# Reordering the turns of a four-layer cross-attention kernel: quotients first, row normalisation on ScalarE

## The chip, the cores and the metric

The kernel runs on one core of a Trainium2 chip. The metric is the device time of one execution in microseconds, the median of several. The core's engines are TensorE (PE; its weight loads are listed apart as PEld), VectorE (DVE), ScalarE (ACT) and GpSimd (POOL). SyncE (SP) issues most of the transfers.

## What is computed

The input x has shape (4, 256, 256): four sequences of 256 tokens with 256 features. Four layers follow each other, and each adds an attention and then a feed-forward part to x:

```python
x = x + xattn(layernorm(x), ctx)      # 16 heads; keys and values are 512 rows of 128 from ctx
x = x + ffn(layernorm(x))             # a different ffn in each layer
```

The attentions of layers 1 to 3 have the form that matters here (layer 0's is smaller and is not touched):

```python
q = (x @ Wq).reshape(B, T, 16, 128); k, v = ctx @ Wk, ctx @ Wv     # 8 key/value groups
out = (softmax(q k^T / sqrt(128)) @ v) @ Wo
```

The feed-forward parts after them are a mixture of eight experts of which each token takes two (layer 1), a choice between two experts (layer 2), and a router that lets 64 tokens of each sequence through an expert (layer 3).

## The kernel before

**Folded weights.** `folding` multiplies Wq with Wk into `m_sb` and Wv with Wo into `n_sb` for each head, in PSUM, and copies the products to SBUF. The copies of the second product are L1006 (64 partitions, two heads) and L1008 (64 partitions, one head, twice).

**The order.** Inside `manual_schedule` each engine executes its instructions in the order of the program text; only the DMA queues are apart. An attention goes through 32 turns, called units: sequence b = 0 to 3, and within it head pair hp = 0 to 7. A turn contains, in this order, pieces of work that belong to different units:

- at hp 1 the statistics of the next sequence's rows (`Norm`), at hp 3 their normalisation (`tokens`, L926);
- the next unit's query products (PE to banks paq and pbq, then L1861 to L1865);
- `row_sums` (L1925, L1926) of the unit that is held back, if there is one;
- `summed` of the previous unit on VectorE (L1978 add, L1980 transposition, L1984 reduction): the denominators of the softmax;
- `exponentials` of this unit: scores on PE into bank "s", exponentials on ScalarE (L1900) into pT;
- at i = 0 (hp 0 and 4) the output products of a finished group of four units;
- `after(b, hp)`: a piece of the following feed-forward part;
- at i = 1 (hp 1 and 5) `quotients` of the last finished group: PE sums into pz (L1993), VectorE inverts (L1999, L2000), multiplies into rr (L2003), reduces (L2004, L2005) and sets signs (L2009);
- for an even hp with b > 0 (a coded unit, but for the second last of a layer): half sums and differences on POOL (L1914, L1920), and the unit is held back for the next turn. For every other unit: `plain` products on PE (L1938 to L1940) into po, copied by ScalarE (L1941);
- at i = 1 and 2 `divided`: VectorE spreads the inverses (L2015, tile wide), POOL multiplies (L2016);
- if a unit is held: `seven_values`, which finishes it with seven products instead of eight: pva on PE (L1950 to L1955), two ScalarE operations (L1956, L1957), pvb on PE (L1963), four VectorE operations (L1967 to L1971). There are 33 such turns, 11 in each layer: hp odd, b > 0, except hp = 7 of b = 3. After it come this unit's own half sums on POOL.

**PSUM banks.** Tiles get banks by tag, in turn: "s" has four, "mm" two, "t" one and "o" one. Scores and output products use "s", queries "mm". The one bank "t" is shared by pz, pva, transposed rows, the routers' small products, and layer 3's gathered rows. The one bank "o" is shared by po and pvb:

```python
pa = bank("t", [P, 2, S], f"pva{L}_{b}_{hp}")
pb = bank("o", [P, 2, S], f"pvb{L}_{b}_{hp}")
```

**The pieces in `after`.** `beside1` (layer 1): for b = 0 it issues waiting weight loads; for b > 0 it does the feed-forward's `Norm` at hp 4, `tokens` at hp 5, transposition at hp 6 and `chosen` at hp 7 (logits pl on PE in bank "t", then some twenty small VectorE operations, L2238 to L2263, and one ScalarE exponential L2244). `beside2` (layer 2) has the same at hp 4 and 5, sends the normalised rows to memory (xd2, on SP's queue), and lets `taken_by` read them; at the last two turns it ranks the tokens and gathers rows with indirect transfers on POOL (L2782). `beside3` (layer 3) does the router: `Norm` at hp 4; `tokens`, `weight` (L3075) and `weights` at hp 5; `spread` and `places` at hp 6 and 7; for b > 1 `gathered` at hp 1 (PE products pxg L3142 in bank "t", copied to xgT by L3149) and `rest` at hp 2 (L3132). With b = 0 it issues loads and takes a step of `bounds` at hp 3, 5 and 7.

The functions of the change with their lines:

Of the kernel before, what the change touches and what calls it, by code (L numbers as in the profile page):

```python
# [12 lines left out]
AF = mybir.ActivationFunctionType  # L13
ALU = mybir.AluOpType
# [3 lines left out]
P = 128  # L18
B, S, D = 4, 256, 256
NC = S // P  # L20
ND = D // P
# [17 lines left out]
KSEL = 64  # L39
# [797 lines left out]
def bounded_path(ctx: ExitStack, tc: tile.TileContext, t, out: bass.AP, over):  # L837
# [70 lines left out]
    class Norm:  # L908
# [11 lines left out]
            nc.vector.tensor_scalar(ve, self.mv[:, :, 1], LN_EPS, None, ALU.add)  # L920
            nc.gpsimd.tensor_tensor(self.rstd, ve, neghalf[:, :NC], ALU.pow)  # L921

        def tokens(self, keep=None):
            xn = keep if keep is not None else lnp.tile([P, NC, D], F32, tag="xn", name=f"xn_{self.name}")
            for c in range(NC):
                nc.vector.tensor_scalar(  # L926
                    xn[:, c, :], x_sb[self.b][:, c, :], self.mv[:, c, 0:1], self.rstd[:, c : c + 1],
                    ALU.subtract, ALU.mult,
                )
            return xn  # L930
# [44 lines left out]
    def folding(L, m_sb, n_sb):  # L975

        for i in range(4):
            h0 = 4 * i
            if (L, i) not in raws:
                load_raw(L, i)  # L980
            wq_t, wk_t, wv_t, wo_t = raws.pop((L, i))
            for g in range(2):
                pm = bank("mm", [P, ND, 2, DC], f"pm_{L}_{i}_{g}")
                for d in range(ND):
                    for h in range(2):
                        nc.tensor.matmul(
                            pm[:, d, h, :],
                            lhsT=wq_t[:, 2 * g + h, d * P : (d + 1) * P],
                            rhs=wk_t[:, g, :],
                            start=True,  # L990
                            stop=True,
                        )
                h1 = h0 + 2 * g
                nc.scalar.mul(m_sb[:, :, h1 : h1 + 2, :], pm, 1.0 / math.sqrt(P))
                m2 = rawp.tile([P, ND, 2, DC], F32, tag="m2", name=f"m2_{L}_{i}_{g}", bufs=1)
                for h in range(2):
                    nc.scalar.activation(
                        m2[:, :, h, :], m_sb[:, :, h1 + h, :], AF.Square,
                        accum_out=msq[:, L - 1, h1 + h : h1 + h + 1],
                    )  # L1000
                pn = bank("mm" if "ring" in banks else "os"[g], [P, 2, D], f"pn_{L}_{i}_{g}")
                nc.tensor.matmul(
                    pn, lhsT=wv_t[:, g, :], rhs=wo_t[:, 2 * g : 2 * g + 2, :], start=True, stop=True
                )
                lo, hi = slice(0, P // 2), slice(P // 2, P)
                nc.vector.tensor_copy(n_sb[hi, h1 : h1 + 2, :], pn[hi])  # L1006
                for h in range(2):
                    nc.vector.tensor_copy(n_sb[lo, h1 + h, :], pn[lo, 1 - h, :])  # L1008
                yield

    def folded(L):
# [742 lines left out]
    def attention(L, m_sb, n_sb, first_xnT=None, after=None, at_end=None, chunk=None, within=None):  # L1754
# [13 lines left out]
        with tc.tile_pool(name=f"att{L}", bufs=2) as ap:  # L1768
# [107 lines left out]
            def coded(b, hp):  # L1876

                return hp % 2 == 0 and 0 < b and (b, hp) != units[-2]
# [186 lines left out]
            for n, (b, hp) in enumerate(units):  # L2065
                if b + 1 < B:
                    if hp == 1:
                        norms[b + 1] = Norm(b + 1, f"a{L}_{b + 1}")
                    elif hp == 3:
                        xns[b + 1] = norms[b + 1].tokens()  # L2070
                if n == 0:
                    first_queries(1)
                    x_sums(0)
                elif n + 1 < len(units):
                    queries(*units[n + 1])
                if b + 1 < B and hp == 5:
                    xnTs[b + 1] = layernorm_T(xns[b + 1], f"a{L}_{b + 1}")
                if b + 1 < B and hp == 6:
                    x_sums(b + 1)
                if b == 0:  # L2080
                    m_sums((hp + 2) % (H // 2))
                if held:
                    row_sums(held[2])
                if n:
                    summed(*units[n - 1], *half)

                last, i = ((b, 0), hp - 4) if hp >= 4 else ((b - 1, 1), hp)
                prev = last[0] >= 0
                h0 = 4 * last[1]
                if prev and i >= 2:  # L2090
                    for k in (2 * i - 4, 2 * i - 3):
                        o_sums(last[0], h0 + k, nc.gpsimd)
                if hp == 0 and b + 1 < B and coded(b + 1, 0) and not coded(b, 0):
                    c_sums(b + 1)
                elif hp == 0 and coded(b, 0) and coded(b - 1, 0):
                    c_sums(b)
                pT = exponentials(b, hp)
                if prev and i == 0 and (b, hp) > (0, 4):
                    out = Output(*((b - 1, 0) if hp == 0 else (b - 1, 1)))
                    out.products()  # L2100
                    out.add()
                if after:
                    after(b, hp)
                if prev and i == 1:
                    quotients(*last)
                if coded(b, hp):
                    h = halves_of(b, hp, pT)
                    held, half = (b, hp, pT, h, differences(b, hp, pT)), (h, None)
                else:
                    plain(b, hp, pT)  # L2110
                if prev and i in (1, 2):
                    for k in (2 * i - 2, 2 * i - 1):
                        divided(last[0], h0 + k, nc.gpsimd)
                if b == 0:
                    n_sums(hp)
                if not coded(b, hp):
                    if held:
                        seven_values(*held)
                        held = None
                    half = halves_of(b, hp, pT), (pT if (b, hp) == units[-1] else None)  # L2120
            out = Output(B - 1, 0)
            summed(*units[-1], *half)
            out.products(lambda: quotients(B - 1, 1))
# [143 lines left out]
    def beside1(b, hp):  # L2267
        if b == 0:
            load_waiting(2)
        if b > 0:  # L2270
            if hp == 4:
                ahead1[b] = Norm(b - 1, f"f1_{b - 1}")
            elif hp == 5:
                ahead1[b] = ahead1[b].tokens()
            elif hp == 6:
                turned1(b - 1, ahead1[b])
            elif hp == 7:
                chosen(b - 1)
# [587 lines left out]
    def beside2(b, hp):  # L2866

        at = 8 * b + hp
        if at == 0:
            backs[2].add()  # L2870
            backs[3].add()
        if at in rows_from:
            backs[rows_from[at]] = Back(rows_from[at])
        if at - 2 in rows_from:
            backs[rows_from[at - 2]].add()
        if at == 16:
            back.close()
            state2["pool"] = f2r.enter_context(tc.tile_pool(name="f2r", bufs=1, side="right"))
        if b == 0:
            load_waiting(1 if hp < 4 else 5)  # L2880
        if b > 0:
            if hp == 4:
                ahead2[b] = Norm(b - 1, f"f2_{b - 1}")
            elif hp == 5:
                xn = ahead2[b].tokens()
                nc.sync.dma_start(xd2[(b - 1) * S : b * S, :].rearrange("(c p) d -> p c d", p=P), xn)
                taken_by(b - 1, xn)
        if b == B - 1:
            if hp == 6:
                ranks2()  # L2890
                places2()
            elif hp == 7:
                for j in range(2):
                    blocks2[j].gather()
                    blocks2[j].weights()
# [163 lines left out]
    class Router:  # L3059
# [5 lines left out]
                self.norm = Norm(b, f"f3_{b}")  # L3065

        def tokens(self):
            self.norm.tokens(xn3[self.b])
            for c in range(NC):
                self.weight(c)  # L3070

# [62 lines left out]
                    ALU.mult, ALU.add,  # L3134
                )

        def gathered(self):
            b = self.b
            px = bank("t", [P, ND, KSEL], f"pxg3_{b}")
            for d in range(ND):  # L3140
                for c in range(NC):
                    nc.tensor.matmul(  # L3142
                        px[:, d, :],
                        lhsT=xn3[b][:, c, d * P : (d + 1) * P],
                        rhs=pick[:, c, b, :],
                        start=(c == 0),
                        stop=(c == NC - 1),
                    )
            nc.vector.tensor_copy(xgT[:, :, b * KSEL : (b + 1) * KSEL], px)  # L3149
# [82 lines left out]
    def beside3(b, hp):  # L3232
# [13 lines left out]
                routers[b - 1].places()  # L3246
        if b > 1:
            if hp == 1:
                routers[b - 2].gathered()
            elif hp == 2:  # L3250
                routers[b - 2].rest()
                if b == 3:
                    picked(0)
# [123 lines left out]
```

## Time and profile before

| quantity | value |
|---|---|
| median of 3 runs (lowest, highest) | 1505.88 us (1502.59, 1506.59) |
| the profiled execution's own time | 1505.62 us |
| its span, first to last instruction | 1503.9 us |
| mean granted TensorE clock | 0.977 |
| PE busy | 1421.1 us (94%), 12555 instructions |
| PEld busy | 975.2 us (65%) |
| DVE busy | 1075.6 us (72%), 2353 instructions |
| POOL busy | 755.7 us (50%), 903 instructions |
| ACT busy | 605.8 us (40%), 1201 instructions |
| layer 1's attention with its turns, 188 to 566 us | PE 364.42 of 378.00 us |
| layer 2's, 640 to 1048 us | PE 381.50 of 408.00 us |
| layer 3's, 1105 to 1470 us | PE 339.29 of 365.00 us |

A line of the list of waits reads: waiting engine, tile and line, what it waited for, total in us, number of times, longest. A line of a timeline reads: start in us, duration in us, engine, line, operation, output and inputs, shape, how many instructions the line stands for, and in brackets the idle time before it and what ended it.

### The profile page before, as it was taken

What the parts mean: (1) busy time and instruction counts of PE and PEld (TensorE: products, weight loads), DVE (VectorE), ACT (ScalarE), POOL (GpSimd) and SP (SyncE); (2) the same over time, 40 slices, a digit from 0 to 9 for tenths busy, and PEclk for the clock granted to TensorE, in tenths of its full rate; (3) what the DMA queues carried; (4) which work ended last, traced back from release to release, by engine and by line L of the source; (5) the groups of instructions that cost most, each with busy time, mean ns of one, the idle gap of its engine ahead of it and who ended that gap; (6) DMA issues with size and microseconds to landing.
All of it is one profiled execution on the core that took longest, in us unless ns stands there. A gap on an engine that the chain in (4) does not pass through costs nothing.

```text
span 1503.9 us, 31066 instructions
## 1 busy us (share of the span) xinstructions
PE 1421.1 (94%) x12555; PEld 975.2 (65%) x12555; DVE 1075.6 (72%) x2353; ACT 605.8 (40%) x1201; POOL 755.7 (50%) x903
## 2 busy tenths in 40 slices
PE   9999999999999999999999898988989998989987
PEld 7665676666665657876666565666855665656656
DVE  5667974677878857547678887766566687777765
ACT  4666453433343432355434343422544333323321
POOL 3222324575666651324587665745133756545650
PEclk9999999999999999999999999999999999999999
DMA  5000221200000002451200000000501000000000
GB/s 155 2 1 2 70 71 39 59 2 9 1 2 8 2 8 56 132 171 43 71 9 9 8 2 8 2 8 15 183 29 47 1 2 1 2 1 2 1 1 31
DMA packets 49492, 47.49 MB, mean 32 GB/s; under 512 B 8282, under 2 KB 45243, under 8 KB 49341
## 3 DMA queue, kind: packets, MB, share of 16 engines
q1 hardware_dynamic: 45740, 37.29, 8.3%
q0 software_dynamic: 2496, 6.82, 1.8%
q8 instruction: 101, 1.65, 0.5%
q10 hardware_dynamic: 1104, 1.31, 0.3%
q14 instruction: 51, 0.41, 0.1%
HBM read 38.60 MB, written 6.82 MB: 30 GB/s over the span
## 4 chain that ended last, share of the span: by engine, by line
PE 66%; DVE 18%; POOL 11%; issue 4%; ACT 1%; POOLq 0%; DVEq 0%
PE ps L1752 12%; POOL half L1914 4%; PE po L1939 4%; PE paq L1752 4%; PE pvb L1963 4%; PE pao L1752 3%; PE pbo L1752 3%; PE pbq L1752 3%; POOL oT L2016 2%; PE pgu L2488 2%; PE ps L1344 2%; PE po L1938 2%; PE po L1940 2%; PE paf L1428 2%; PE pyf L1478 2%
## 5 line engine op out<-in xcount | busy, mean ns | idle before, releaser
L1752 PE MATMUL ps<-qT,cT 128*64 128x512 f32 x1536 | 347.8, 593 | 0.0
L1900 ACT ACTIVATE pT<-ps,mbias 128x512 f32<-128x512 f32 x384 | 260.6, 687 | 162.4 <-PE ps L1752 126.2
L1914 POOL TENSOR_TENSOR half<-pT 128x1024 f32<-128x1024 f32 x93 | 220.0, 2366 | 96.6 <-ACT pT L1900 67.3
L1939 PE MATMUL po<-pT,c_sb 128*64 128x512 f32 x504 | 229.5, 598 | 0.0
L1752 PEld LDWEIGHTS ps<-qT,cT 128*64 128x64 f32 x1536 | 117.6, 137 | 157.8 <-issue 153.0
L2016 POOL TENSOR_TENSOR oT<-oT,wide 128x512 f32<-128x512 f32 x90 | 117.4, 1324 | 191.4 <-DVE wide L2015 191.4
L1938 PE MATMUL po<-pT,c_sb 128*64 128x256 f32 x504 | 152.1, 383 | 0.0
L1940 PE MATMUL po<-pT,c_sb 128*64 128x256 f32 x504 | 150.8, 381 | 0.0
L1941 ACT COPY oT<-po 128x512 f32<-128x512 f32 x63 | 36.8, 585 | 186.7 <-PE po L1940 186.7
L1940 PEld LDWEIGHTS po<-pT,c_sb 128*64 128x64 f32 x504 | 69.4, 138 | 38.9 <-issue 0.8
L1938 PEld LDWEIGHTS po<-pT,c_sb 128*64 128x64 f32 x504 | 66.8, 138 | 27.1 <-issue 8.0
L1348 ACT ACTIVATE pT<-ps 128x512 f32<-128x512 f32 x128 | 65.9, 604 | 32.9 <-PE ps L1344 32.7
L1939 PEld LDWEIGHTS po<-pT,c_sb 128*64 128x64 f32 x504 | 66.3, 137 | 16.0 <-issue 9.0
L1978 DVE TENSOR_TENSOR half<-half 128x512 f32<-128x512 f32 x63 | 46.2, 733 | 39.4 <-POOL half L1914 33.8
L1752 PE MATMUL paq<-xnT_a,m_sb 128*64 128x128 f32 x720 | 73.5, 273 | 0.0
L1752 PE MATMUL paq<-xx,m_x 128*64 128x128 f32 x720 | 73.2, 273 | 0.0
L1963 PE MATMUL pvb<-pT,cx 128*64 128x256 f32 x528 | 72.3, 419 | 0.5 <-DVE pT L1926 0.5
L1861 ACT COPY qT<-paq 128x128 f32<-128x128 f32 x90 | 23.9, 265 | 116.9 <-PE paq L1752 116.6
L1984 DVE TENSOR_REDUCE sums<-turned 128x16 f32<-128x512 f32 x96 | 65.9, 686 | 3.3
L1752 PE MATMUL pao<-n_x,ox 128*64 128x128 f32 x672 | 67.7, 273 | 0.0
L1950 PE MATMUL pva<-dT,cx 128*64 128x256 f32 x132 | 24.2, 443 | 44.7 <-DVE rr L2003 40.9
L921 POOL TENSOR_TENSOR rstd_f<-ve_f,neghalf 128x2 f32<-128x2 f32 x15 | 10.6, 704 | 110.1 <-DVE ve_f L920 61.6
(495 smaller groups left out, 3410.7 us busy)
## 6 DMA issues: line engine op xcount, KB each, us to landing
wq<-in_L_wqT SPq DMA_DIRECT2D x11, 512.0 KB
wo<-in_L_wo SPq DMA_DIRECT2D x11, 512.0 KB
yd<-yr SPq DMA_DIRECT2D x23, 128.0 KB
w<-in_F_w SPq DMA_DIRECT2D x4, 512.0 KB
xd<-xn_f SPq DMA_DIRECT2D x7, 256.0 KB
wk<-in_L_wkT SPq DMA_DIRECT2D x11, 128.0 KB
wv<-in_L_wvT SPq DMA_DIRECT2D x11, 128.0 KB
x_sb<-in_x SPq DMA_DIRECT2D x4, 256.0 KB
```

The costliest lines, as they stand in the source:

```text
L1348: nc.scalar.activation(pT[kp][:, j], ps[j], AF.Exp)
L1752: nc.tensor.matmul(out[r], lhsT=lhsT[:, r], rhs=rhs, start=start, stop=stop)
L1900: done["head"] = nc.scalar.activation(pT[:, k, :], ps, AF.Exp, bias=mbias[:, b, k : k + 1]).ins
L1914: nc.gpsimd.tensor_tensor(half, pT[:, 0:2], pT[:, 2:4], ALU.add)
L1938: nc.tensor.matmul(po[LO, :S], lhsT=c_lo, rhs=pT[:, k, S:], start=(k == 0), stop=False)
L1939: nc.tensor.matmul(po[HI], lhsT=c_hi, rhs=pT[:, k], start=(k == 0), stop=last)
L1940: nc.tensor.matmul(po[LO, S:], lhsT=c_lo, rhs=pT[:, k, :S], start=False, stop=last)
L1941: nc.scalar.copy(raw_of(b, hp), po)
L1963: nc.tensor.matmul(pb[r, j], lhsT=cx[:, p, i, :], rhs=rhs, start=(p == 0 and j == 0), stop=(p == 1 and j == 1),)
L1978: nc.vector.tensor_tensor(part, half[:, 0], half[:, 1], ALU.add)
L1984: nc.vector.tensor_reduce(sums[b, hp // 4][:, hp % 4, :], turned, AX.X, ALU.add)
L2016: eng.tensor_tensor(outs[b, hp], outs[b, hp], wide.rearrange("p f i -> p (f i)"), ALU.mult)
```

## The change

It has four parts.

1. `tokens(on_act=True)`: instead of two VectorE operations that subtract the mean and multiply by the inverse deviation, one VectorE operation on 128x2 makes shift = -mean x rstd (in place of the mean), and two ScalarE Identity activations with scale and bias pointers write the rows. It is used at hp 3 for the next sequence's own rows, and at hp 5 for the feed-forward parts of layers 1, 2 and 3.
2. In a turn with a held unit, `summed` moves from behind `row_sums` to behind `quotients`, and `after` follows it. In other turns `summed` stays. `after` keeps about its old place in held turns and in even turns with b > 0; in all turns with b = 0, and in the last turn of b = 3, it moves to the end of the turn, behind this unit's half sums.
3. `gathered` at hp 1 of layer 3 takes a bank "mm" instead of "t".
4. In `folding`, one copy with a reversed read takes the place of two.

```diff
-        def tokens(self, keep=None):
+        def tokens(self, keep=None, on_act=False):
             xn = keep if keep is not None else lnp.tile([P, NC, D], F32, tag="xn", name=f"xn_{self.name}")
+            if on_act:
+                shift = self.mv[:, :, 0]
+                nc.vector.scalar_tensor_tensor(shift, shift, -1.0, self.rstd, ALU.mult, ALU.mult)
+                for c in range(NC):
+                    nc.scalar.activation(
+                        xn[:, c, :], x_sb[self.b][:, c, :], AF.Identity, bias=shift[:, c : c + 1],
+                        scale=self.rstd[:, c : c + 1],
+                    )
+                return xn
...
-                for h in range(2):
-                    nc.vector.tensor_copy(n_sb[lo, h1 + h, :], pn[lo, 1 - h, :])
+                nc.vector.tensor_copy(n_sb[lo, h1 : h1 + 2, :], pn[lo, ::-1, :])
...
-                        xns[b + 1] = norms[b + 1].tokens()
+                        xns[b + 1] = norms[b + 1].tokens(on_act=True)
...
                 if held:
                     row_sums(held[2])
-                if n:
+                elif n:
                     summed(*units[n - 1], *half)
...
-                if after:
-                    after(b, hp)
                 if prev and i == 1:
                     quotients(*last)
+                if held:
+                    summed(*units[n - 1], *half)
+                early = held or (b and hp % 2 == 0)
+                if after and early:
+                    after(b, hp)
...
                     half = halves_of(b, hp, pT), (pT if (b, hp) == units[-1] else None)
+                if after and not early:
+                    after(b, hp)
...
-                ahead1[b] = ahead1[b].tokens()
+                ahead1[b] = ahead1[b].tokens(on_act=True)
...
-                xn = ahead2[b].tokens()
+                xn = ahead2[b].tokens(on_act=True)
...
-            self.norm.tokens(xn3[self.b])
+            self.norm.tokens(xn3[self.b], on_act=True)
...
-        def gathered(self):
+        def gathered(self, tag="t"):
             b = self.b
-            px = bank("t", [P, ND, KSEL], f"pxg3_{b}")
+            px = bank(tag, [P, ND, KSEL], f"pxg3_{b}")
...
-                routers[b - 2].gathered()
+                routers[b - 2].gathered("mm")
```

## The prediction

> **What bounds the kernel now.** I read the page's busy shares first, then TensorE's waits, then the timelines of the turns those waits lie in. TensorE (PE) is busy 1421.1 of 1503.9 us, so at most 82.8 us of waiting can go. The waits of PE (us in total, times, longest):
>
> ```profile
> PE pva L1950 <- DVE rr L2003: 40.9, 11, 5.7
> PE pz L1993 <- DVE sums L1984: 5.8, 2, 5.2
> PE pz L1993 <- DVE xgT L3149: 2.2, 2, 1.8
> ```
>
> Half of all idle time is one wait: pva takes PSUM bank "t", which pz holds until VectorE (DVE) has read it at L2003. Nine of the eleven are hp5 turns of b=1..3, about 2.7 us in layer 1, 5.2 in layer 2, 4.4 in layer 3: 37.5 us by the bracketed idle times of the nine starts; two hp1 turns have 1.54 and 1.85. VectorE in one such turn:
>
> ```profile
> 366.31 0.68 DVE L1926 TENSOR_TENSOR pT<-pT 128x512 f32<-128x512 f32 x1
> 366.92 0.68 DVE L1978 TENSOR_TENSOR oT<-half 128x512 f32<-128x512 f32 x1
> 367.63 0.71 DVE L1980 STREAM_TRANSPOSE turned<-oT 128x512 f32<-128x512 f32 x1
> 368.38 0.69 DVE L1984 TENSOR_REDUCE sums<-turned 128x16 f32<-128x512 f32 x1
> 368.98 0.73 DVE L926 TENSOR_SCALAR xn_f<-x_sb,mv_f,rstd_f 128x256 f32<-128x256 f32 x2
> 369.62 0.22 DVE L1999 TENSOR_SCALAR rz<-pz 128x64 f32<-128x64 f32 x1
> 369.87 0.55 DVE L2000 RECIPROCAL rz<-rz 128x64 f32<-128x64 f32 x1
> 370.46 0.19 DVE L2003 TENSOR_TENSOR rr<-pz,rz 128x32 f32<-128x32 f32 x1
> ```
>
> The quotients (L1999 to L2003) stand behind the sums and the row normalisation. On PE and ScalarE (ACT) of that turn:
>
> ```profile
> 367.56 0.59 PE L1940 MATMUL po<-pT,c_sb 128*64 128x256 f32 x2
> 370.80 0.65 PE L1950 MATMUL pva<-dT,cx 128*64 128x256 f32 x4 [2.65 <-DVE rr L2003]
> 372.12 3.61 PE L1963 MATMUL pvb<-pT,cx 128*64 128x256 f32 x16
> 368.19 0.59 ACT L1941 COPY oT<-po 128x512 f32<-128x512 f32 x1 [2.98 <-PE po L1940]
> ```
>
> pvb needs bank "o", which the copy L1941 empties; it is done at 368.8, long before 372.12. That matters below.
>
> **What the Trainium skill says.** "TensorE: Matmul & The Clock Gate", section "What's actually happening", says an idle window of about 3.4 us halves the PE clock. The trace shows the effect after shorter gaps: after the nine hp5 waits weight loads take 232 ns instead of 137, and pva to the next step takes 4.5 to 6.0 us against 3.02 in unstalled turns, 18.7 us over the nine. Gaps of 2.40 and less mostly leave the clock alone. "ScalarE: Activation LUTs", "What ACT_TABLE_LOAD costs", prices an ACTIVATE at 186 ns + 0.833 ns per element, + 93 ns per pointer operand, 93 ns overlapped. For Identity with two pointers on 512 that is 0.80; L1333 shows 0.79. From that row, 0.79 - 256 x 0.000833 = 0.58 us at 256, my estimate for each new one. "SBUF — State Buffer", "Who interferes with whom", calls the port pair of VectorE and GpSimd (POOL) an exclusive lock: whoever starts first blocks the other, if the VectorE operation has two SBUF inputs. The trace agrees:
>
> ```profile
> 337.92 2.35 POOL L1914 TENSOR_TENSOR half<-pT 128x1024 f32<-128x1024 f32 x1
> 337.93 3.77 DVE L926 TENSOR_SCALAR xn_a<-x_sb,mv_a,rstd_a 128x256 f32<-128x256 f32 x2
> ```
>
> Two passes of 0.40 each took 3.77 because POOL had started 10 ns earlier. Small ones are blocked too: L920 on 128x2 took 2.34 instead of 0.17.
>
> **The hp5 turns (nine).** Let S be the end of row_sums (L1926, 366.95 here). Removed: VectorE's two normalising passes (0.73) and, from in front of the quotients, summed (2.06). The quotients free bank "t" at S+1.2. The plain products end at S+1.2 (b=1, 2) or S+0.5 (b=3), so pva waits 0 or 0.7. Added: a shift of 128x2 on VectorE (0.2) and two Identities on ScalarE, in `after`, which comes before the plain copy L1941 in ScalarE's order. The shift comes after quotients and summed: S + 1.5 + 2.1 + 0.2 = S+3.8. Two Identities, 1.1, and the copy, 0.6, give S+5.5, while pva is through at S+1.2+1.3 = S+2.5. So a **new wait of 3.0 us before pvb** takes the old one's place, long enough for the slow clock, 1.6 us (near the least of the nine, as work was done in between). Queued behind the copy are ScalarE's copies of pva, which are not late. Per turn 4.6 us (three with 0.7 more), 43.5 in all, for 37.5 + 18.7 = 56.2: **-12.7** (layer 1 -0.6, layer 2 -7.6, layer 3 -4.5). POOL is idle in this turn from 365.84 (end of its dT) to L2016 at 371.89, so this shift is not blocked. Behind the Identities VectorE waits about 1.1 us in layers 2 and 3, where taken_by (four operations) and the router's weight (two, L3075) read xn; next on its queue is the transposition L2015 for POOL's L2016. It started at S+4.15 in layer 1 and about S+6.4 in layer 2, and would start at S+4.0 and near S+6.5, as the removed 0.73 pays for most of the wait; so POOL is not late, cost 0. If POOL were later by 1 us, its next half sum would hold the next turn's products by as much. The transfer of xn to xd2 in layer 2 is issued from SP after the Identities; its reader comes turns later. Cost 0; if that cover went, the gathers of the last turn would move by the same 1 to 2 us.
>
> **The hp3 turns (six with b=1, 2).** Tokens stands first in the turn: shift, then ScalarE's Identities ahead of the copies and exponentials:
>
> ```profile
> 338.71 0.69 ACT L1900 ACTIVATE pT<-ps,mbias 128x512 f32<-128x512 f32 x1 [1.25 <-PE ps L1752]
> 341.04 0.38 PE L1938 MATMUL po<-pT,c_sb 128*64 128x256 f32 x1
> ```
>
> The shift has two SBUF inputs. It wants to start where L926 starts, which in five of the six such turns is 10 to 20 ns behind L1914. Blocked, it ends near 340.4, the Identities at 341.5, the first exponential at 342.2 to 342.3, and the plain products start about 1.25 later than 341.04. Unblocked, the exponential ends near 340.0 and nothing waits. I take blocked, since POOL runs straight on from its previous operation and wins each time. Price: three turns x 1.25 = +3.75. In the b=1 turns of layers 1 and 2 the 1.54 and 1.85 gained at hp1 are lost again, since POOL's chain has not moved, and the stall of 2.8 or more brings 1.4 of slow clock: net +2.65 each, **+5.3**. Layer 3, b=2: L926 started at 1314.29 behind L3132, the first exponential at 1311.95; it would end some 3.2 late, with clock 1.5, less 0.5 saved later: **+4.2**. From both sides, these six are worth between -3.4 + 4.2 = +0.8 (unblocked, hp1's gain kept) and +19 (slow clock in all, layer 3's stall 4 us).
>
> **Layer 3, hp1.** `gathered` in bank "mm": pz no longer waits for xgT: 2.24 us and 1.4 of slow clock, **-3.6**. "mm" has two banks for the queries, so the next query products could wait 0 to 0.5 us.
>
> **The layers' last turns.** Layer 1: the logits pl and some twenty small VectorE operations (563.44 to 567.4) ran beside the plain products. Placed last they start at about 566.5; the last summed ends near 573.2 instead of 570.2, PE waits 2.9 with a little clock, less waits that it hides: **+3.1**. Layer 2: POOL's two gathers (L2782, 2.6 us from 1032.50) move behind the half sum L1912, which starts at once; the last pz waited 5.24 at half clock, and now about 2.5: **-4.0**. Layer 3: +0.3. In the b=0 turns `after` moves to the end of the turn: its SP and POOL loads are issued up to a turn later but are needed a layer later; bounds' 2.4 us wait stays. 0, within 1 either way.
>
> **Folding copy.** Two of 64x256 at 0.41 become one of 64x512 at 0.695 (L1006): 24 x 0.13 of VectorE, hidden behind the folding matmuls but for one 2.0 us wait: **-0.1**.
>
> **Sum.** -12.7 - 3.6 + 3.75 + 5.3 + 4.2 + 3.1 - 4.0 + 0.3 - 0.1 = -3.75. The profiled execution took 1505.62 (span 1503.9, 1.7 around it), 0.26 under the median 1505.88: 1501.9 on it, **1502** on the median.
>
> **Rivals.**
> - *Shift not blocked.* If it starts ahead of L1914, hp3's nine us go and hp1's 3.4 stay: -12.4 more, about 1489.5. For: an operation of 0.17 started 8 ns ahead of POOL once (L2248 at 564.51) and ran free; retimed turns may flip the order. Against: the five starts above.
> - *ScalarE's copy not late.* If ScalarE held nothing back, pva and pvb follow at once: 56.2 saved instead of 12.7, some 1458. Against: ScalarE's queue is strict FIFO (the skill's clock-gate page, "Architectural detail"; the trace's ScalarE rows follow program order). The change would then do what its order suggests.
> - *The clock decides (slower).* The new stalls fall at hp3 and before pvb, a place with no stall now. If slow stretches there are 2.3 instead of 1.6 at nine hp5 sites (+6.3; 2.9 were seen) and come at the three hp3 sites where I counted none (+4.2), the sum is +6.75: 1512.6. It decides from 0.31 us more per site at twelve sites.
> - *The wait only changes its name.* Layer 1's -0.6 everywhere: about +8, in the same place as the last; for it, the copy is late by the same queue; against, layers 2 and 3 have two-fold longer waits now.
>
> **Chances.** Base case, blocked, 0.43 (1495 to 1509); unblocked 0.31; copy not late 0.04; slower two together 0.20; nothing measurable changed 0.02. About 0.3% (4.5 us) can be told from no change. Faster: 0.43 x 0.44 + 0.30 + 0.04 = 0.53. Slower: 0.43 x 0.12 + 0.16 = 0.21. Within: 0.26. The base case's own range is 1495 to 1509; to hold eight in ten it goes from 1484, below the unblocked case, to 1513.
>
> **What would show it.** Right: pva <- rr gone or under 3 us in all; a new wait of pvb on L1941 or its bank, about nine times 3 us; Identities of 0.58 us; po waiting for pT at hp3; pz <- xgT gone; 5.2 of pz <- sums halved in layer 2, a new one near 3 us in layer 1. Wrong: no pvb wait (then far below 1490), no po wait at hp3 (1490), or Identities well above 0.6.

## The result and the profile after

The changed kernel takes 1497.08 us (median of 5 runs, 1496.41 to 1501.05), the kernel before 1505.46 (median of 5): 8.4 us less, ratio 0.9956 with a 95% interval of 0.9938 to 0.9974. The forecast was 1502 in a range of 1484 to 1513. The profiled execution took 1496.82, with a span of 1494.9. The changed file has its lines 8 to 13 further down: pva is L1958, pvb L1971, the plain copy L1949, rr L2011, the half sums L1922, wide L2023, POOL's product L2024, the exponentials L1908.

TensorE's waits of the kernel after (total, times, longest):

```profile
PE pvb L1971 <- ACT oT L1949: 23.3, 9, 2.6
PE pz L2001 <- DVE sums L1992: 6.9, 3, 3.2
PE pao L1760 <- ACT pT L1908: 5.0, 4, 1.5
PE po L1946 <- ACT pT L1908: 4.2, 2, 4.0
...
PE pva L1958 <- DVE rr L2011: 2.3, 4, 0.7
```

The wait of 40.9 us is down to 2.3 (for rr), and pz no longer waits for xgT. But over half of it stands again one step later: nine waits of pvb for the plain copy. Two kinds are new in the attentions, pao (a tile of the output products) and po on the exponentials. Over the whole span TensorE idles 78.5 us, 4.3 less than before, and is busy 1416.4, 4.7 less. It executes the same instructions, so this second half of the gain is clock: the mean granted clock was 0.984 in the profiled execution, and 0.977 before. The turn shown in the prediction (layer 1, b=1, hp5) now reads, on VectorE, ScalarE and TensorE:

```profile
366.74 0.19 DVE L2011 TENSOR_TENSOR rr<-pz,rz 128x32 f32<-128x32 f32 x1
...
368.72 0.69 DVE L1992 TENSOR_REDUCE sums<-turned 128x16 f32<-128x512 f32 x1
369.33 0.15 DVE L927 SCALAR_TENSOR_TENSOR mv_f<-mv_f,rstd_f 128x2 f32<-128x2 f32 x1
369.39 1.30 DVE L2023 STREAM_TRANSPOSE wide<-rz 128x512 f32<-128x512 f32 x2
```

```profile
369.57 1.09 ACT L929 ACTIVATE xn_f<-x_sb,mv_f,rstd_f 128x256 f32<-128x256 f32 x2 [5.40 <-DVE mv_f L927]
370.57 0.56 ACT L1949 COPY oT<-po 128x512 f32<-128x512 f32 x1
```

```profile
367.08 0.65 PE L1958 MATMUL pva<-dT,cx 128*64 128x256 f32 x4
371.19 3.39 PE L1971 MATMUL pvb<-pT,cx 128*64 128x256 f32 x16 [2.60 <-ACT oT L1949]
```

Read across: rr is done 2.5 us before the sums are, and pva starts with no idle time in brackets. ScalarE sits 5.40 us idle with the Identities at the head of its queue, because they need the shift (369.33), and the copy that frees bank "o" stands behind them. That is the hand-over that the prediction worked out, with a wait of 2.6 us where it had 3.0.

**Where the 9.0 us of span went.** The same TensorE instructions stand in both traces, so the difference of their start times shows where the kernels part. Each row is the step of that difference over the turn, clock included:

| place | forecast, us | measured, us |
|---|---|---|
| ahead of layer 1's turns | -0.1 | -0.8 |
| nine hp5 turns | -12.7 | -19.3 (layer 1: 0.0, -1.6, -1.3; layer 2: -5.0, -4.1, -2.3; layer 3: -1.3, -2.4, -1.2) |
| hp1 of layers 1 and 2, b=1 | in the next row | -1.8, -1.5 |
| hp3, five turns | +9.05 | +0.5 in one, else 0 |
| hp4, four turns (pao waits for the exponentials) | none | +1.3, +1.5, +1.7, +1.3 |
| hp6 in layer 2 (paq waits for xx and xnT_a) | none | +1.3, +1.2 |
| layer 3, hp1 | -3.6 | -3.6, -0.6 |
| layer 3, b=2, hp3 | +4.2 | +5.1 |
| layer 3, hp7 | none | +0.3, +0.8 |
| end of layer 1, then its feed-forward | +3.1, 0 | +2.9, +1.4 |
| end of layer 2 | -4.0 | -1.8 |
| end of layer 3 | +0.3 | +1.7 |

They add up to about -8.5; the rest is steps below 0.4 us. The feed-forward of layer 1 has the same program in all kernels here, and in the trace of order_only (below) its step is +5.4, so the +1.4 may be chance.

### The profile page after: what moved, and what is told of

Same layout as the page of the kernel before. It is cut to its first block, busy times and chain, and to the rows that moved or that the text cites. A ratio compares the mean times of both kernels' runs of the same rounds, so it can differ in the third digit from the quotient of the medians.

```text
span 1494.9 us, 31072 instructions
## 1 busy us (share of the span) xinstructions
PE 1416.4 (95%) x12555; PEld 967.0 (65%) x12555; DVE 1061.8 (71%) x2311; ACT 620.4 (42%) x1237; POOL 756.6 (51%) x903
## 4 chain that ended last, share of the span: by engine, by line
PE 33%; POOL 9%; DVE 9%; issue 3%; ACT 1%; DVEq 0%; POOLq 0%; ACTq 0%
PE ps L1760 8%; POOL half L1922 4%; PE po L1947 3%; PE pao L1760 2%; PE pbo L1760 2%; PE paq L1760 2%; POOL oT L2024 2%; PE pbq L1760 2%; PE po L1946 1%; PE pvb L1971 1%; PE po L1948 1%; PE py L1760 1%; PE pb L2828 1%; DVE pT L1933 1%; PE pm L995 1%
## 5 line engine op out<-in xcount | busy, mean ns | idle before, releaser
L1908 ACT ACTIVATE pT<-ps,mbias 128x512 f32<-128x512 f32 x384 | 258.1, 688 | 162.1 <-PE ps L1760 112.0
L1922 POOL TENSOR_TENSOR half<-pT 128x1024 f32<-128x1024 f32 x93 | 219.9, 2365 | 86.8 <-ACT pT L1908 55.1
L2024 POOL TENSOR_TENSOR oT<-oT,wide 128x512 f32<-128x512 f32 x90 | 122.6, 1381 | 189.6 <-DVE wide L2023 189.6
L1949 ACT COPY oT<-po 128x512 f32<-128x512 f32 x63 | 36.7, 582 | 153.0 <-PE po L1948 153.0
L1971 PE MATMUL pvb<-pT,cx 128*64 128x256 f32 x528 | 70.8, 414 | 23.3 <-ACT oT L1949 23.3
L1971 PEld LDWEIGHTS pvb<-pT,cx 128*64 128x64 f32 x528 | 43.0, 148 | 45.3 <-ACT oT L1949 27.4
L1870 DVE TENSOR_TENSOR qT<-qT,paq 128x128 f32<-128x128 f32 x90 | 25.0, 278 | 59.6 <-ACT qT L1869 59.3
```

The costliest lines, as they stand in the source:

```text
L1908: done["head"] = nc.scalar.activation(pT[:, k, :], ps, AF.Exp, bias=mbias[:, b, k : k + 1]).ins
L1922: nc.gpsimd.tensor_tensor(half, pT[:, 0:2], pT[:, 2:4], ALU.add)
L1949: nc.scalar.copy(raw_of(b, hp), po)
L1971: nc.tensor.matmul(pb[r, j], lhsT=cx[:, p, i, :], rhs=rhs, start=(p == 0 and j == 0), stop=(p == 1 and j == 1),)
L2024: eng.tensor_tensor(outs[b, hp], outs[b, hp], wide.rearrange("p f i -> p (f i)"), ALU.mult)
```

## The experiments

All times are medians with the ratio to the kernel before, measured beside it on the same chip.

**One part alone.** `order_only` is the kernel before with the new order within the turns alone (`after` is not moved to the end of any turn), `act_only` with ScalarE's rows alone.

```diff
 order_only
-                if n:
+                elif n:
                     summed(*units[n - 1], *half)
...
-                if after:
-                    after(b, hp)
                 if prev and i == 1:
                     quotients(*last)
+                if held:
+                    summed(*units[n - 1], *half)
+                if after:
+                    after(b, hp)
 act_only: tokens(on_act=True) at its four callers, nothing else
```

> The kernel before with one part of the change: in held turns quotients, then summed, then after. No ScalarE rows, no late last turns, bank t for gathered, two folding copies. If this order alone carries the gain: like rows_dve (1493) less what the other small parts bring, 1494 to 1499. If ScalarE's rows or the small parts carry it: 1502 to 1506.

> The kernel before with the other part: all rows by ScalarE, in the old order. The quotients still stand behind summed and the shift, so the waits of pva for rr stay within 0.6 us each of before (40.9 us in all, 33 to 41 now), the copy is done before pvb wants its bank, and layer 3's po waits 4 us for pT: 1503 to 1511. If ScalarE carried the gain of the change: below 1500.

`order_only`: 1497.52, 0.9941 (0.9924 to 0.9957), the whole change's gain within the intervals; its four executions spread from 1494.38 to 1503.62, and the profiled one is the slowest of them. `act_only`: 1512.39, 1.0055 (1.0038 to 1.0071), slower than before. TensorE's waits of act_only show why:

```profile
PE pva L1959 <- DVE rr L2012: 41.4, 11, 6.0
PE pz L2002 <- DVE sums L1993: 5.8, 2, 5.2
PE py L1761 <- POOL oT L2025: 3.1, 4, 1.0
PE po L1947 <- ACT pT L1909: 3.0, 1, 3.0
```

The first row is what it was: in layer 1 each wait at hp5 shrinks by 0.6 us, and in layers 2 and 3 each grows by 0.3 to 0.4, since VectorE there waits 0.7 us for the Identities. Layer 3's po waits on top: that turn loses 5.4 us by the start times, of 6.7 in all. So the order carries the gain, and the rows on ScalarE are no part of it. The smaller parts (`after` at the end of turns, the bank of gathered, the folding copy) were not run one by one; with the order they make up rows_dve below.

**ScalarE's rows taken back, and the copy put first.**

```diff
 rows5_dve: the three feed-forward callers (hp5) without on_act
 rows3_dve: the attention's own rows (hp3) without on_act
 rows_dve:  both
 copy_first
+                behind = held and hp == 5
-                if after and early:
+                if after and early and not behind:
                     after(b, hp)
...
                     plain(b, hp, pT)
+                    if after and behind:
+                        after(b, hp)
```

> Only ScalarE's order in the nine hp5 turns differs from the changed kernel: the plain copy (L1949) comes ahead of the two Identities. Theory A (the Identities hold the copy, and the copy holds pvb's bank): the nine waits of pvb, 23.3 us, and the slow clock behind them, 9.8 us by pva to the next step against 3.02, go; 33 us less, about 1464. Theory B (POOL's chain of half sums is next, so what PE wins at hp5 it waits for again at hp6 to hp1, as it did in layer 2 with 3.0 of 5.1 and 2.7 of 4.1 us): at most 10 less, about 1487. Both at work: about half, 1480.

> The rows of hp5 are normalised on VectorE as before (two operations of 0.4 us behind the sums); all else as in the changed kernel. Theory A: no wait of pvb for the copy, the same 33 us less or a little more, since VectorE no longer waits 1.1 us for Identities in layers 2 and 3 (paq on xx, 2.5 us, goes too): about 1462, so at hp5 ScalarE's share in the change would be a loss. Theory B: at most 10 less, 1487. If ScalarE's part were what brought the gain: slower than 1497.

> The rows of hp3 are normalised on VectorE as before; all else as in the changed kernel. If the shift on ScalarE's path costs PE (the 4.0 us wait of po for pT in layer 3, and through earlier row_sums that collide with POOL's L2024, the four waits of pao for pT, 5.0 us): 4 to 10 less, about 1490. If Identity on ScalarE frees VectorE where it matters: 3 to 8 more, since L926 is blocked for 3.8 us again and row_sums come later.

> All rows on VectorE as before; what is left of the change is the order, the bank of gathered and the folding copy. Theory A: the two before add up, about 1455 to 1462. Theory B: 1480 to 1490. If the gain needs ScalarE: above 1497.

Measured: `copy_first` 1498.65, 0.9954 (0.9939 to 0.9969); `rows5_dve` 1500.33, 0.9964 (0.9951 to 0.9977); `rows3_dve` 1496.63, 0.9934 (0.9909 to 0.9958); `rows_dve` 1493.11, 0.9910 (0.9887 to 0.9933). My theory A falls: the copy is no longer held in copy_first, all nine waits of pvb are gone, and nothing is won. The expected times were missed too: copy_first and rows5_dve came out 11 us or more above theory B's limit, rows3_dve won nothing of the 4 to 10 us, and rows_dve lies above B's 1480 to 1490. A rows5_dve above 1497 was to mean that ScalarE's part brings the gain; rows_dve, which has none of it and is the fastest of the four, speaks against that. Its interval lies clear of those of copy_first and rows5_dve, not of rows3_dve's. TensorE's waits of copy_first:

```profile
PE pz L2001 <- DVE sums L1992: 9.0, 3, 3.4
PE paq L1760 <- DVE xx L1792: 6.0, 6, 1.3
PE pva L1958 <- POOL ox L1786: 5.5, 2, 3.2
PE paq L1760 <- DVE qT L1872: 4.7, 4, 1.9
PE po L1946 <- ACT pT L1908: 4.2, 2, 4.0
PE pva L1958 <- DVE sc L2259: 3.8, 2, 1.9
```

Of the 23.3 us, 19.3 came back as other waits (TensorE idles 74.5 us, where it was 78.5), most of them for VectorE and POOL in the next two turns. The clock did not gain either: TensorE is busy 1422.0 us, 5.6 more, at a mean clock of 0.980 where the changed kernel had 0.984 (0.979 to 0.981 in all six executions). What one sees in layer 1, b=1: pvb starts 2.5 us earlier than in the changed kernel, and as it runs at full clock the lead grows to 4.0; paq gives back 1.4 at hp6, pva gives back 1.6 at hp7, and 1.0 is left. The busy times from hp5 to hp7 of that sequence in copy_first (stretch, its length, then busy us of PE, PEld, VectorE, ScalarE, POOL, granted clock, DMA share, GB/s) say who is next:

```profile
366.50:390.00 23.50, 20.65 (x168) 12.31 (x166) 20.95 (x44) 9.72 (x18) 18.91 (x22) 1.00 0.04 13
```

VectorE is as busy there as TensorE, and at the same place in layers 2 and 3 busier (23.06 and 21.53 of 25.00 us, 24.48 and 22.71 of 27.00). Part of this busy time is itself waiting for POOL, as the next experiments show. rows5_dve stays behind rows_dve by 7.2 us. In its trace the Identities at hp3 bring one wait of po in layer 3, of 3.98 us, that rows_dve doesn't have. Another 4.3 us of difference between these two traces are clock: at hp7 of layer 1, b=1 and 2, pva waits 3.1 us in both, and a slow stretch follows in one only.

**Is it VectorE, or POOL?** Three kernels take VectorE's four x_sums of hp6 (sums of the next sequence's rows, tile xx) away from it at b=1 and 2: two give them to POOL at hp5, one leaves them out.

```diff
 x_pool, copy_first_x_pool
-            def x_sums(b):
+            def x_sums(b, eng=nc.vector):
...
-                t_sums(nc.vector, *x_blocks(b), *(xxs[b][:, i, :] for i in range(3)))
+                t_sums(eng, *x_blocks(b), *(xxs[b][:, i, :] for i in range(3)))
...
                     xnTs[b + 1] = layernorm_T(xns[b + 1], f"a{L}_{b + 1}")
+                    if b:
+                        x_sums(b + 1, nc.gpsimd)
-                if b + 1 < B and hp == 6:
+                if b + 1 < B and hp == 6 and not b:
                     x_sums(b + 1)
 copy_first_no_x
                 if b + 1 < B and hp == 6:
-                    x_sums(b + 1)
+                    if b:
+                        xxs[b + 1] = xxs[1]
+                    else:
+                        x_sums(b + 1)
```

> As copy_first, and the sums x_sums of the next sequence's rows (four VectorE operations at hp6, b=1 and 2) go to POOL at hp5, where POOL has nothing to do for 6 us. If VectorE's chain from hp5 to hp7 is what took copy_first's gain back: the waits of paq for xx (6.0 us) and xnT_a (2.2 us) go, 5 to 9 less than copy_first, about 1491. If POOL's chain of half sums is next: the same waits turn into waits of pva for ox or of pao, 0 to 2 less, 1497 or more.

> The changed kernel with x_sums on POOL at hp5 alone; the copy still stands behind the Identities. Only the waits on xx and xnT_a are there to be won (1.8 us), since the wait of pvb hides the rest: 0 to 2 less than 1497. If instead VectorE's time at hp6 counts by itself: 5 or more less.

> As copy_first, with x_sums of b=2 and 3 left out (those of b=1 are read in their place), so some 2.0 us of VectorE work at hp6 are gone in two sequences of each layer and no other engine gets them. If VectorE's time from hp5 to hp7 is what took copy_first's gain back: the waits of paq for xx and xnT_a (8.2 us) go and those of pva at hp7 (9.3 us) shrink by most of 2 us each, 9 to 14 less than copy_first, about 1487. If POOL's chain of half sums holds the turns: 0 to 3 less, 1496 or more.

Measured: `copy_first_x_pool` 1502.21, 0.9969 (0.9957 to 0.9981); `x_pool` 1499.82, 0.9964 (0.9950 to 0.9979); `copy_first_no_x` 1499.30, 0.9966 (0.9956 to 0.9977). None beats copy_first: VectorE's chain alone isn't the bound either. For the two with the copy first these are the times that were expected if POOL's half sums hold the turns; wide_first, below, tests that. The profiled execution of copy_first_no_x took 1505.29, 6 us above its median, so differences of its times are rough. In it the waits for xx and xnT_a are gone, and VectorE reaches row_sums of hp7 1.3 us sooner (381.30 for 382.64, of which 0.5 comes from earlier turns). This is what it meets (VectorE, then POOL):

```profile
381.30 1.75 DVE L1933 TENSOR_TENSOR pT<-pT 128x512 f32<-128x512 f32 x1 [0.71 <-POOL half L1922]
382.97 1.76 DVE L1934 TENSOR_TENSOR pT<-pT 128x512 f32<-128x512 f32 x1
384.66 1.75 DVE L1986 TENSOR_TENSOR oT<-half 128x512 f32<-128x512 f32 x1
```

```profile
378.89 2.38 POOL L1922 TENSOR_TENSOR half<-pT 128x1024 f32<-128x1024 f32 x1
381.22 1.28 POOL L1928 TENSOR_TENSOR dT<-pT 128x512 f32<-128x512 f32 x1
382.44 3.42 POOL L2024 TENSOR_TENSOR oT<-oT,wide 128x512 f32<-128x512 f32 x2
```

First it waits for POOL's half sums, and then three additions of 0.68 take 1.75 each, while POOL's dT and its two products run at the same time (the products take 3.42 instead of 2.5). POOL works here without a pause from 370 to 390 us. Its stretch after hp1 is 22.4 us long in the kernel before, after and copy_first alike; it begins when `wide` is there.

**Bank "t" at hp7, and the last turns.**

```diff
 rows_dve_mm7: rows_dve, and
-        pl = bank("t", [P, NC, NE], f"pl_{b}")
+        pl = bank("mm", [P, NC, NE], f"pl_{b}")
...
-        def places(self):
+        def places(self, tag="t"):
...
-            pp = bank("t", [P, NC], f"pp3_{b}")
+            pp = bank(tag, [P, NC], f"pp3_{b}")
...
-                routers[b - 1].places()
+                routers[b - 1].places("mm")
 mm7_early7: rows_dve_mm7, and
-                early = held or (b and hp % 2 == 0)
+                early = held or (b and (hp % 2 == 0 or L != 2))
```

> As rows_dve, and at hp7 the logits pl of layer 1 and the counts pp of layer 3 take a bank mm instead of t. If the waits of pva at hp7 (6.2 us for sc, 5.5 us that the list puts to ox) are waits for bank t, which VectorE reads late: they go, up to 12 less, with half of it back at the next exponentials 6 less, about 1487. If pva waits for POOL there, as the list says of ox: those 5.5 us stay, 1490 or more.

> As rows_dve_mm7, with after back ahead of the plain products in the last turn of b=3 in layers 1 and 3 (layer 2 keeps it late). By the traces the late place cost 2.9 us in layer 1 and 1.6 in layer 3: 3 to 5 less than rows_dve_mm7, about 1483. If those were only clock: the same as rows_dve_mm7.

Measured: `rows_dve_mm7` 1494.35, 0.9917 (0.9890 to 0.9945), no gain over rows_dve, where 6 to 12 us were expected; `mm7_early7` 1489.23, 0.9892 (0.9862 to 0.9923). It is the fastest of all, and its interval lies below the changed kernel's. Of TensorE's waits of rows_dve, these two stood at hp7:

```profile
PE pva L1958 <- DVE sc L2256: 6.2, 2, 3.1
PE pva L1958 <- POOL ox L1786: 5.5, 2, 3.2
```

In rows_dve_mm7 both are gone, also the one that the list puts to POOL's ox, so both were waits for bank "t". In their places stand

```profile
PE pp L3126 <- DVE qT L1872: 5.8, 2, 2.9
...
PE pvb L1971 <- ACT oT L1949: 4.9, 2, 2.5
```

and the time did not change. `after` early in the last turns of layers 1 and 3 gave 5.1 us between the medians, near the 3 to 5 that were expected, though the two intervals overlap. The traces are 6.2 us apart, and little of that is waiting: pz waits 1.3 less in layer 1, and all idle time is 1.2 less (71.5 for 72.7). The other 5.0 are TensorE's busy time, 1414.9 for 1419.9, with a mean clock of 0.986 for 0.982. That the late place costs clock, rather than that the clock fell out well in these executions, is not shown.

**POOL's stretch begun earlier.**

```diff
 wide_first: mm7_early7, and
+                soon = held and prev and i == 1
                 if prev and i == 1:
                     quotients(*last)
+                if soon:
+                    for k in (0, 1):
+                        divided(last[0], h0 + k, nc.gpsimd)
                 if held:
                     summed(*units[n - 1], *half)
...
-                if prev and i in (1, 2):
+                if prev and i in (1, 2) and not soon:
```

> As mm7_early7, and at i=1 of held turns the two transpositions into wide (L2023) come straight behind quotients, ahead of summed and after. Theory C: POOL starts its unbroken stretch of work at hp5 (8.9 to 29 us long, the same length in every kernel so far) and at hp1 (22.4 us) only when wide is there, and the end of that stretch holds the exponentials and hp7; so 2.1 us earlier at hp1, 2.8 earlier in layer 1's hp5 and about 4.4 in layers 2 and 3. The waits that are left there (paq 8.2, pp 5.8, pvb 4.9, pao 6.1 us) shrink: 5 to 15 less than mm7_early7, about 1479. If VectorE's own chain holds those turns: 0 to 2 less, or up to 5 more, since summed comes 1.3 later and its addition meets POOL's L2024 at the shared ports.

Measured: 1501.05, 0.9959 (0.9944 to 0.9975), some 10 us slower than mm7_early7 by the ratios, where 5 to 15 less or at most 5 more was expected. My next theory (C in the expectation) falls as well. POOL did start earlier: its idle time ahead of `wide` fell from 6.1 to 4.0 us at hp1, and at hp5 from 5.9, 8.3 and 7.4 in layers 1, 2 and 3 to 3.3 in each. But VectorE's two row operations and the addition of summed now run beside it (layer 2, VectorE and POOL):

```profile
829.92 1.38 DVE L1986 TENSOR_TENSOR oT<-half 128x512 f32<-128x512 f32 x1
...
832.75 2.61 DVE L935 TENSOR_SCALAR xn_f<-x_sb,mv_f,rstd_f 128x256 f32<-128x256 f32 x2
```

```profile
832.39 2.35 POOL L1922 TENSOR_TENSOR half<-pT 128x1024 f32<-128x1024 f32 x1
```

L935 took 0.73 in this place in mm7_early7. The delay reaches the query sums: TensorE's waits of wide_first begin with

```profile
PE paq L1760 <- DVE qT L1872: 16.1, 6, 5.0
```

against 3.1 before this edit. The waits at which theory C aimed did go (pp 5.8 and pvb 4.9 us) or shrink (pao on pT from 3.9 to 2.2), and at the start of layer 2 the trace of wide_first is 1.1 us ahead; the loss falls in layers 2 and 3. In the traces it is 3.5 us of idle time (75.0 for 71.5) and 6.2 of busy time, at a clock of 0.979 for 0.986.

## Why the prediction was right, and where it was not

The range and the sign held, and the sum missed by 5 us. That it came so near is in part luck. By the table above, the hp5 turns came out 6.6 us better than forecast and hp1 with hp3 11.9 better, while costs that were put at nothing or too low add up to some 15 us the other way. Point by point:

**The wait moves from pva to pvb: right.** Nine waits of 2.58 to 2.60 were measured where 3.0 was forecast; the copy ends at S+5.1 instead of S+5.5, the shift being ready at S+3.4. Mis-sized is the slow clock: 1.6 us in each turn was counted, but three of the nine (layer 1 b=2, layer 2 b=1 and 2) run on at full clock, with 0.3 us lost. Over the nine turns the shorter waits are worth 3.6 us (9 x 0.4) and the milder clock 4.6 (pva to the next step takes 60.2 us in all; less 9 x 3.02 and the waits of 23.3 that leaves 9.8, for 14.4 counted); some 1.7 of this is lost again in the same turns. So the third rival, a slower clock behind these waits, had the sign wrong.

**hp3 "blocked": wrong.** In five of six turns nothing was held, as in the first rival. In layers 1 and 2, b=1, the shift ran ahead of POOL's half sum, as that rival supposed. In the other three it started 11 to 18 ns behind it, where L926 had started 10 to 20 ns behind and lost; the shift did not lose (layer 1, b=2):

```profile
422.96 0.12 DVE L927 SCALAR_TENSOR_TENSOR mv_a<-mv_a,rstd_a 128x2 f32<-128x2 f32 x1
```

```profile
422.94 2.37 POOL L1922 TENSOR_TENSOR half<-pT 128x1024 f32<-128x1024 f32 x1
```

The step that failed is that the small shift, so close behind POOL, is held as operations of 128x256 were. Its size alone did not free it. In the three b=0 turns of the same trace the same shift starts some 260 ns behind POOL and is held to the end of POOL's operation (layer 1):

```profile
260.63 2.10 DVE L927 SCALAR_TENSOR_TENSOR mv_a<-mv_a,rstd_a 128x2 f32<-128x2 f32 x1
```

```profile
260.37 2.35 POOL L1922 TENSOR_TENSOR half<-pT 128x1024 f32<-128x1024 f32 x1 [4.16 <-ACT pT L1908]
```

The prediction's own example of a small one, L920 with 2.34 us, had started 44 ns behind POOL. That example and L926 are TENSOR_SCALAR operations with one input tile besides scalars, so they do not bear out its condition of two SBUF inputs either; what they show is that they were held. In layer 3, b=2, where the shift took 0.83, the 4.0 us wait was right, since it hangs on L3132's two passes ahead of it.

**The rival's 1489.5 did not come.** The step "hp1's 3.4 stay" failed, for the reason that I gave for the other case, POOL's chain, one turn later. With L926 out of the way, row_sums meet POOL's L2024 at the ports (3.41 instead of 2.55), and POOL's half sums of hp3 start only 0.7 us earlier, while TensorE is 2.4 earlier. The exponentials of hp4 wait for that half sum, and pao for the exponentials:

```profile
340.65 3.41 POOL L2024 TENSOR_TENSOR oT<-oT,wide 128x512 f32<-128x512 f32 x2
...
348.27 2.37 POOL L1922 TENSOR_TENSOR half<-pT 128x1024 f32<-128x1024 f32 x1
```

```profile
350.66 2.42 ACT L1908 ACTIVATE pT<-ps,mbias 128x512 f32<-128x512 f32 x4 [3.67 <-POOL half L1922]
```

That is four times 1.1 to 1.5 us. "POOL is not late, cost 0" at hp5 failed in the same way for VectorE: L2023 and all behind it come at the old distance to row_sums in layer 2, so what TensorE gains there it partly gives back at hp6 (xx and xnT_a, 2.5 us in two turns).

**The second rival (1458)** was the largest misjudgement, though it had a chance of 0.04: copy_first is that case, with the copy not late, and takes 1498.65. Its 56 us were never there, as only the waits on TensorE were counted.

**The ends.** Layer 1 (+2.9 for +3.1) and layer 3's hp1 (-4.2 for -3.6) were right. Layer 2 gave 1.8 instead of 4.0: pz waited 3.2 instead of 2.5 and half clock followed as before. **ScalarE's Identities:** 1.09 for two, 1.1 by the working; the trace has eight table loads, as before.

**What stays open.** In copy_first TensorE, VectorE and POOL are busy 20.65, 20.95 and 18.91 of the 23.50 us from hp5 to hp7, and the last two hold each other up. Less work on VectorE gave waits for POOL, an earlier POOL gave waits for VectorE. What relieving both at once would bring was not tried, so that the two together are the bound is argued and not shown. Nor is it settled what rows on ScalarE cost in the new order: at hp3 they cost 7.2 us where the hp5 rows are on VectorE and 0.5 where those are on ScalarE; at hp5 they cost 3.5 where the hp3 rows are on VectorE, and less than nothing where those are on ScalarE. Past the one wait in layer 3 these differences are near the width of the intervals. And the clock is open: in the traces it makes up half of the change's gain and much of the differences between the variants, and what decides whether a wait is followed by a slow stretch was not found.

## What to carry to other kernels

A stall on the busiest engine may cover work of its neighbours that is nearly as long: before pricing the stall as a gain, add up each neighbour's busy time over the same two or three turns, and if one of them fills them, count only the difference (this is drawn from copy_first; no run tests it as a rule). Moving an operation to an idle engine also moves it into that engine's order; ask what stands behind it there and what it must itself wait for. Split the time saved into idle time and busy time of that engine: where the instructions are the same, a change of the busy time is clock, and no list of waits shows it. And an edit of several parts is best measured part by part: here one part brought all of the gain, and another one alone made the kernel slower.

## What the runs showed of the hardware

A VectorE operation on 128x2 with two SBUF inputs ran in 0.12 us in three places of the changed kernel where POOL had started a 2.4 us operation 11 to 18 ns earlier (422.96 beside 422.94), while operations of 128x256 at 10 to 20 ns were held (3.77 us for two of 0.40). The same small operation was held for 2.1 us in three other places, where it started some 260 ns behind POOL. In the traces of the variants it went free at up to 23 ns (copy_first_x_pool) and was held at 53 (1.23 us, act_only). So the distance in time counts here, and not the size or kind of the operation alone. Where both engines have several such operations in a row both lose: three additions of 0.68 took 1.75 each, and POOL's pair 3.4 instead of 2.5. And nine idle times of TensorE of equal length, 2.58 to 2.60 us, were followed by a slow stretch in six cases and by full clock in three, so a gap of this size has no fixed price.
